# Four cross-attention layers on one core: where the small-head attention groups stand in the order of the program

## The chip, the cores and the metric

The kernel runs on one core of one Trainium2 chip. The metric is the device time of one execution in microseconds (us). Everything is float32. The engines of the core are named as the profile names them: PE (TensorE, matmuls; PEld is its weight load), DVE (VectorE), ACT (ScalarE), POOL (GpSimd) and SP (SyncE, which here only issues DMAs). Each engine works its own instructions in the order of the program and waits for semaphores of others.

## The reference, cut to what matters

Four attention layers follow each other on a state `x` of 4 batches x 512 rows x 256 columns. All four attend to the same context (4 x 1024 x 512). Layers 0, 2 and 3 are alike; layer 1 is another form.

```
# layers 0, 2, 3 ("masked"): 16 heads of 64
q, k, v = x @ Wq, ctx @ Wk, ctx @ Wv
logits  = q k^T / 8 + col_bias        # bias on up to 4 key columns, from two masks over the rows
x       = softmax(logits) v @ Wo + bo + x

# layer 1 ("grouped"): 16 query heads of 16, 4 key/value heads, each shared by 4 query heads
xn      = rmsnorm(x) * norm_w
q, k, v = xn @ wq, ctx @ wk, ctx @ wv
x       = x + softmax(q k^T / 4) v @ wo
```

Layer l+1 of a batch needs layer l of that batch whole; different batches don't depend on each other.

## The kernel before

**Groups.** Work comes in groups (`units`, L44). A masked group is two heads of one layer and one batch: 8 groups a layer, 96 in all. A grouped group of layer 1 is two key/value heads (h = 0 or 1) for one of the four query heads r that share them: 8 for each batch, 32 in all, in the order r0h0, r0h1, r1h0 and so on. For each group 8 tiles of scores, 128 keys x 1024 (two heads x 512 queries), are made, reduced to a maximum over all keys, diminished by it, put through the exponential and multiplied with v.

**Order.** Two strings give the order by hand: character n of `MASKED_TURNS` (L57) is the batch whose next masked group runs in step n, and character n of `GROUPED_TURNS` (L61) is the batch whose next grouped group has its second half in step n, or "." for none. The loop at L1020 runs over the steps n = 0 to 97. In this text step n begins on PE with the first matmul of its masked scores (L692), and steps are told apart by that. In step n there are:

- `g`, the masked group of step n: scores (L692; L698 adds the bias), copied out of PSUM by ACT (L702), maximum by DVE (L706, then `max_quarters` L743 to L758 and `max_everywhere` L769), subtraction on DVE (L777), exponentials on ACT (L783), a running sum of the exponentials on POOL (L822);
- `g1`, the masked group of step n-1: its product with v on PE (`attend`, L722) and `normalise` on DVE (L743 to L868);
- `lam`, the grouped group of step n: subtraction on POOL (L775), exponentials on ACT, its product with v on PE (also L722), `keep_even`/`keep_odd` and, for h = 1, `turn_grouped` (L732 to L839);
- `coming`, the grouped group of step n+1: its scores in four pairs of tiles (`logits_pair`, L669), copied by ACT (L675), maximum by DVE (L681, then as above into L769);
- projections as filling between these: `project_q` (L610), for odd n the keys of the next two masked groups (L514, 32 matmul records in the trace, listed as 8 items by `keys`), for even n their values (L553, 64 records, 8 items by `values`), and `project_out` (L886), whose result DVE adds to the state (L904 or L908). For two masked groups at a time it stands first in the filling of odd steps (`outs`).

So a grouped group has its first half (`coming`) in the step before its own and its second half (`lam`) in its own. In the order before, the 8 grouped groups of a batch stand in consecutive steps (12 to 19, 22 to 29, 32 to 39, 68 to 75), and inside such a block every step has both a `lam` and a `coming`. The step two before a block makes the keys of layer 1 and the norm (`k_grouped` L532, `rms_norm` L649), the step just before it their values (`v_quarter` L576).

**The filling list.** Each entry has a supposed time, which are summed in `now`. Pair 0 of the `coming` scores is put in where `now` reaches 12.0 with a `lam` or 11.0 without; the next three follow 2.5 apart. Before pair 0 `behind_exponentials` sends out everything else that the step still holds: all subtractions, exponentials and `normalise(g1)`. `attend_grouped` (the `lam` product) is put in where 9.5 is reached.

**PSUM.** The 8 banks are given out by `Place` (L101), for one bank or an aligned pair of banks, the longest returned first. This happens in the order of the program, so a matmul that gets a bank waits until the last reader of that bank is done. A pair of grouped score tiles takes two aligned pairs of banks.

**State.** `x_all` (L343) holds four states of 512 KB. A new state is taken when a masked layer's first `project_out` runs and returned when its last `project_q` has run (`new_state`, `drop_state`). `part_x` (L365) loads a batch's input.

**Queue of SP.** All loads of weights and of the context go through SP in program order: `load_masked` at the head of a step, `load_others` at its end. `fetch_half` brings the context of a batch (two halves of 1 MB) when the batch of the masked groups changes.

Of the kernel before, what the change touches and what calls it, by code (L numbers as in the profile page):

```python
# [8 lines left out]
FP = mybir.dt.float32  # L9
# [7 lines left out]
P = 128  # L17
B, S, C = 4, 512, 256
# [3 lines left out]
KC = C // P  # L22
# [21 lines left out]
def units(b):  # L44
# [10 lines left out]


MASKED_TURNS = (  # L57
    "000000001111111122222222000000001111111100000000"
    "222222223333333311111111222222333333332233333333"
)  # L60
GROUPED_TURNS = (  # L61
    "............00000000..11111111..22222222........"
    "....................33333333...................."
)


CONTEXT_STEPS = ((1, 2, 3, 4), (5, 5, 6, 6), (7, 7, 8, 8))


# [11 lines left out]
def kernel(ctx: ExitStack, tc: tile.TileContext, a: dict, out: bass.AP):  # L81
    nc = tc.nc

    def pool(name, **kw):
        return ctx.enter_context(tc.tile_pool(name=name, bufs=1, **kw))
# [3 lines left out]
    dr = pool("dr", space=bass.MemoryType.DRAM)  # L89
# [43 lines left out]
    def give_set(g):  # L133
        sets_free.append(g.set)
# [186 lines left out]
    xs = {}  # L321
# [24 lines left out]
    def new_state(l, b):  # L346
        x_at[l, b] = x_free.pop(0)
        xs[l, b] = x_all[:, x_at[l, b]]
        return xs[l, b]

    def drop_state(l, b):
        x_free.append(x_at[l, b])

    def load_parts(b, first):

# [74 lines left out]
    def w_tile(g, n, kk, bufs):  # L430
        return t_([P, kk, P], f"w{n}", f"w{n}_{g.name}", bufs=bufs)
# [20 lines left out]
    def load_grouped(g, n):  # L452


        if n == "k":
            w = t_([P, NT, P], "v1", f"wk_{g.name}")[:, 0:KT, :]
        else:
            w = t_([P, S], "o1", f"wv_{g.name}").rearrange("p (k c) -> p k c", c=P)
        g.w[n] = w
        nc.gpsimd.memset(w, 0.0)  # L460
        for k in range(KT):
            nc.sync.dma_start(
                out=w[:, k, :].rearrange("p (g d) -> p g d", d=32)[:, :, 0:16],
                in_=a[f"L1_xattn_w{n}"][k * P : (k + 1) * P, :].rearrange("p (g d) -> p g d", d=16),
            )

    def load_q(g):
        if g.masked:
            g.wq = w_tile(g, "q", KC, 2)
            nc.sync.dma_start(  # L470
                out=g.wq,
                in_=a[f"L{g.l}_xattn_Wq"][:, g.p * P : (g.p + 1) * P].rearrange("(k p) c -> p k c", p=P),
            )
        elif g.h == 0:
            g.wq = w_tile(g, "q1", KC, 1)
            nc.gpsimd.memset(g.wq, 0.0)
            for k in range(KC):
                nc.sync.dma_start(
                    out=g.wq[:, k, :].rearrange("p (g d) -> p g d", d=32)[:, :, 0:16],
                    in_=a["L1_xattn_wq"][k * P : (k + 1) * P, :].rearrange(  # L480
                        "p (g r d) -> p g r d", r=4, d=16
                    )[:, :, g.r, :],
                )

    def load_o(g):
        if g.masked or g.h == 1:
            g.wo = t_([P, C], "wo", f"wo_{g.name}", bufs=4)
        if g.masked:
            nc.sync.dma_start(out=g.wo, in_=a[f"L{g.l}_xattn_Wo"][g.p * P : (g.p + 1) * P, :])
        elif g.h == 1:  # L490
            nc.gpsimd.memset(g.wo, 0.0)
            for i in range(4):
                at = 64 * i + 16 * g.r
                nc.sync.dma_start(out=g.wo[32 * i : 32 * i + 16, :], in_=a["L1_xattn_wo"][at : at + 16, :])
# [8 lines left out]
    def k_part(g, n, part):  # L503

        if not g.masked:
            return k_grouped(g, n, part)
        if n == 0 and part == 0:
            g.kt = t_([P, T], "kt", f"kt_{g.name}", bufs=2)
        if part == 0:
            g.k_place = Place(1)  # L510
        w = g.k_place
        m = w.ap
        for k in (2 * part, 2 * part + 1):
            nc.tensor.matmul(  # L514
                m, lhsT=g.w["k"][:, k, :], rhs=ctx_half[g.b, n][:, k, :],
                start=(k == 0), stop=(k == KT - 1),
            )
        if part:
            return lambda: (nc.scalar.copy(g.kt[:, n * 512 : (n + 1) * 512], m), w.back())  # L519
# [188 lines left out]
    def place_out(g, width=1):  # L708
        g.place = Place(width)
        g.po, g.psum = g.place.ap[:, 0:S], g.place.ap[:, S:]  # L710
# [16 lines left out]
    def keep_even(g):  # L727


        if g.h == 0:  # L730
            gq[g.b, "o"] = t_([P, S], "o1", f"o1_{g.name}")
        nc.scalar.copy(gq[g.b, "o"][64 * g.h : 64 * (g.h + 1), :], g.po[0:64, :])  # L732

    def keep_odd(g):
        half = gq[g.b, "o"][64 * g.h : 64 * (g.h + 1), :]
        nc.vector.tensor_tensor(half, half, g.po[64:128, :], ALU.add)  # L736
        g.place.back()
# [86 lines left out]
    def turn_grouped(g):  # L824
        w = Place(1)
        normalise_grouped(g, w.ap)
        w.back()
# [113 lines left out]
    masked = [g for g, _ in steps if g]  # L941
    step_of = {(g.l, g.b, g.u): n for n, both in enumerate(steps) for g in both if g}
# [3 lines left out]
    def at(n):  # L946
        return steps[n] if 0 <= n < len(steps) else (None, None)
# [8 lines left out]
    def head(g):  # L956
        return steps[step_of[1, g.b, 0]][1]
# [8 lines left out]
    for b in range(B):  # L966
        first = next(g for g in masked if (g.b, g.l, g.u) == (b, 0, 0))
        for n, part_of in enumerate(load_parts(b, first.n == 0)):
            at_step = -1
            if first.n:  # L970
                before = masked[first.n - 2]
                at_step = step_of[before.l, before.b, before.u] - 1
                if n < 4:
                    at_step = CONTEXT_STEPS[b - 1][n]
            parts.setdefault(at_step, []).append(part_of)

    def run(items):
# [25 lines left out]
    def keys(*of):  # L1003
        return [
            (1.7, lambda h=h, part=part, each=each: k_part(each, h, part))
            for h in range(2) for each in of for part in range(2)
        ]

    def values(of):
        if of.masked:  # L1010
            return [(1.8, lambda n=n, h=h: v_pair(of, n, h)) for n in range(NI) for h in range(2)]
        return [(1.8, lambda h=h, part=part: part(of, h)) for h in range(2) for part in (v_begin, v_end)]
# [7 lines left out]
    for n in range(len(steps) + 2):  # L1020
        g, lam = at(n)
        follows, coming = at(n + 1)
        soon = at(n + 2)[1]
        g1, attended = attended, g
        ending = n >= len(steps) - 2

        rests = [p() for p in parts.get(n, ())] if n >= 0 else []
        kk = []
        if g:
            kk = masked[1:2] if n == 0 else masked[g.n + 1 : g.n + 3] if g.n % 2 else []  # L1030
# [17 lines left out]
        def load_others():  # L1048
            third = at(n + 3)[1]
            if third and third.first:  # L1050
                load_grouped(third, "k")
            if coming and coming.h == 1 and soon:
                load_q(soon)
            if soon and soon.first:
                load_q(soon)
                load_grouped(soon, "v")
            if coming:
                load_o(coming)
# [80 lines left out]
        if coming:  # L1139
# [6 lines left out]
        fill, of_grouped = (  # L1146
            [
                (1.8 * len(each), lambda each=each: project_out(*each))
                for each in outs if each[0].masked == m
            ]  # L1150
            for m in (True, False)
        )
        outs = []
        fill += [(1.7, lambda each=each: project_q(each)) for each in queries]
        if kk:
            fill += keys(*kk)
        of_values = values(g) if g and g.n % 2 == 0 else []
        fill += of_values[:4] + of_grouped + of_values[4:]
        if lam:

            def attend_grouped():
                while any(of is lam for _, of, _ in events):
                    events.pop(0)[2]()
                lam.v = head(lam).v
                place_out(lam)
                attend(lam)
                give_set(lam)
                late.append(lambda: keep_odd(lam))
                if lam.h == 1:
                    late.append(lambda: turn_grouped(lam))  # L1170
                return lambda: keep_even(lam)

            total, where = 0.0, 0
            while where < len(fill) and total < 9.5:
                total += fill[where][0]
                where += 1
            fill.insert(where, (3.6, attend_grouped))
        if soon and soon.first:
# [5 lines left out]
            of_keys = keys(soon)  # L1184
# [37 lines left out]
        if n == 0:  # L1222
            load_masked()
        load_others()
        for b in range(B):
            if left[b] == 0:
                left[b] = -1
                store(b)
# [23 lines left out]
```

## Time and profile before

| | us |
|---|---|
| median of 3 runs | 3630.98 (3629.69 to 3631.89) |
| the profiled execution, its own time | 3630.16 |
| its span in the trace | 3628.1 |

The mean granted clock of TensorE over the span is 0.995 of full speed. Some groups of the page that the steps are built of, with their mean durations:

| what | engine, line | count | mean ns |
|---|---|---|---|
| subtraction, masked | DVE L777 | 768 | 1215 |
| maximum, masked | DVE L706 | 672 | 1232 |
| maximum, grouped | DVE L681 | 224 | 1233 |
| maximum over a tile's quarters | DVE L743 (scores) | 128 | 1265 |
| spreading the maximum, grouped | DVE L769 | 32 | 1246 |
| adding a projection to the state | DVE L908 | 52 | 1218 |
| copy of a score tile, masked / grouped | ACT L702 / L675 | 768 / 256 | 1048 / 1015 |
| exponential of a tile | ACT L783 | 1024 | 1058 |
| running sum | POOL L822 | 668 | 2365 |
| subtraction, grouped | POOL L775 | 256 | 2371 |

A mean for PE is not the pace at which matmuls follow each other, since they overlap: the chain of waits has stretches of 13.73 us for 32 of L514 (0.429 us each) and 13.81 us for 64 of L553 (0.216 us each). The moving operand of both is float32, with 512 and 256 columns.

### The profile page before, as it was taken

What the parts mean: (1) busy time and instruction counts of PE and PEld (TensorE: products, weight loads), DVE (VectorE), ACT (ScalarE), POOL (GpSimd) and SP (SyncE); (2) the same over time, 40 slices, a digit from 0 to 9 for tenths busy, and PEclk for the clock granted to TensorE, in tenths of its full rate; (3) what the DMA queues carried; (4) which work ended last, traced back from release to release, by engine and by line L of the source; (5) the groups of instructions that cost most, each with busy time, mean ns of one, the idle gap of its engine ahead of it and who ended that gap; (6) DMA issues with size and microseconds to landing.
All of it is one profiled execution on the core that took longest, in us unless ns stands there. A gap on an engine that the chain in (4) does not pass through costs nothing.

```text
span 3628.1 us, 40560 instructions
## 1 busy us (share of the span) xinstructions
PE 3551.9 (98%) x14510; PEld 1708.9 (47%) x14510; DVE 3022.2 (83%) x4134; ACT 2313.0 (64%) x2657; POOL 2220.0 (61%) x1005
## 2 busy tenths in 40 slices
PE   8999999999999999999999999999999999999998
PEld 4554444444444444444545454454444445454554
DVE  7877789887889878998888888888788888888787
ACT  4565577775777667776555555555577765555554
POOL 3565477775677757776555545455577775545454
PEclk9999999999999999999999999999999999999999
DMA  3231101011100110001001001011101101002100
GB/s 89 61 110 62 56 27 41 21 31 43 46 22 22 43 46 22 22 22 42 26 27 50 28 28 50 27 50 30 44 22 46 28 19 50 27 20 71 33 31 6
DMA packets 159373, 140.01 MB, mean 39 GB/s; under 512 B 42424, under 2 KB 142264, under 8 KB 158660
## 3 DMA queue, kind: packets, MB, share of 16 engines
q1 hardware_dynamic: 153518, 124.32, 11.1%
q0 software_dynamic: 2560, 8.39, 0.8%
q10 hardware_dynamic: 3094, 4.72, 0.6%
q8 instruction: 114, 1.87, 0.2%
q14 instruction: 87, 0.71, 0.1%
HBM read 122.71 MB, written 10.49 MB: 37 GB/s over the span
## 4 chain that ended last, share of the span: by engine, by line
PE 72%; DVE 19%; ACT 6%; issue 2%; ACTq 0%; DVEq 0%; DMA 0%; POOL 0%; POOLq 0%
PE ps L514 16%; PE ps L553 15%; PE ps L722 14%; PE ps L692 14%; DVE ps L706 7%; DVE st L777 4%; PE ps L610 4%; PE ps L669 3%; ACT st L783 3%; PE ps L886 3%; DVE ps L743 2%; DVE ps L681 1%; DVE ps L769 1%; ACT st L675 1%; DVE every L758 1%
## 5 line engine op out<-in xcount | busy, mean ns | idle before, releaser
L822 POOL TENSOR_TENSOR st<-st 128x1024 f32<-128x1024 f32 x668 | 1580.0, 2365 | 1058.1 <-ACT st L783 1013.2
L783 ACT ACTIVATE st<-st 128x1024 f32<-128x1024 f32 x1024 | 1035.8, 1058 | 465.9 <-DVE st L777 399.5
L706 DVE TENSOR_TENSOR ps<-ps,st 128x1024 f32<-128x1024 f32 x672 | 828.0, 1232 | 367.9 <-ACT st L702 307.8
L777 DVE TENSOR_TENSOR st<-st,ps 128x1024 f32<-128x1024 f32 x768 | 881.2, 1215 | 3.4
L722 PE MATMUL ps<-st,v 128*64 128x512 f32 (+1 forms) x4064 | 801.5, 595 | 9.2 <-ACT st L783 9.2
L775 POOL TENSOR_TENSOR st<-st 128x1024 f32<-128x1024 f32 x256 | 596.8, 2371 | 313.3 <-DVE st L769 195.7
L702 ACT COPY st<-ps 128x1024 f32<-128x1024 f32 x768 | 716.3, 1048 | 96.5 <-PE ps L698 67.1
L692 PE MATMUL ps<-qt,kt 64*128 64x512 f32 x3072 | 718.1, 599 | 26.4 <-DVE ps L743 19.6
L514 PE MATMUL ps<-ctx,wk 128*128 128x512 f32 x1536 | 695.4, 603 | 2.2 <-ACT ctx L416 2.2
L553 PE MATMUL ps<-wv,ctx 128*128 128x256 f32 x3072 | 687.6, 381 | 0.0
L553 PEld LDWEIGHTS ps<-wv,ctx 128*128 128x128 f32 x3072 | 578.7, 190 | 144.0 <-issue 69.0
L722 PEld LDWEIGHTS ps<-st,v 128*64 128x64 f32 (+1 forms) x4064 | 241.6, 130 | 550.9 <-issue 430.3
L692 PEld LDWEIGHTS ps<-qt,kt 64*128 64x128 f32 x3072 | 300.4, 186 | 386.7 <-issue 147.7
L514 PEld LDWEIGHTS ps<-ctx,wk 128*128 128x128 f32 x1536 | 288.3, 191 | 393.1 <-issue 364.1
L681 DVE TENSOR_TENSOR ps<-ps,st 128x1024 f32<-128x1024 f32 x224 | 276.1, 1233 | 74.2 <-ACT st L675 61.2
L675 ACT COPY st<-ps 128x1024 f32<-128x1024 f32 x256 | 247.5, 1015 | 83.8 <-PE ps L669 82.0
L616 ACT ACTIVATE qt<-ps 128x512 f32<-128x512 f32 x96 | 56.6, 589 | 317.0 <-PE ps L610 317.0
L519 ACT COPY kt<-ps 128x512 f32<-128x512 f32 x192 | 111.2, 579 | 179.3 <-PE ps L514 170.6
L669 PE MATMUL ps<-qt,kt 32*128 32x512 f32 x1024 | 184.4, 645 | 18.7 <-DVE o L736 10.1
L610 PE MATMUL ps<-x,wq 128*128 128x512 f32 x384 | 187.4, 611 | 1.1 <-ACT x L379 1.1
L886 PE MATMUL ps<-ot,wo 128*128 128x512 f32 x384 | 177.9, 606 | 0.7 <-DVE ot L868 0.7
L743 DVE TRANSPOSE_TENSOR_REDUCE ps<-ps 128x32 f32<-128x1024 f32 x128 | 162.0, 1265 | 12.5 <-PE ps L692 0.5
(142 smaller groups left out, 1650.7 us busy)
## 6 DMA issues: line engine op xcount, KB each, us to landing
ctx<-kept SPq DMA_DIRECT2D x24, 1024.0 KB, 8.4
wk<-in_L_xattn_Wk_dram SPq DMA_DIRECT2D x47, 512.0 KB, 3.6
wv<-in_L_xattn_Wv_dram SPq DMA_DIRECT2D x47, 512.0 KB, 3.7
wq<-in_L_xattn_Wq_dram SPq DMA_DIRECT2D x96, 128.0 KB, 3.5
wo<-in_L_xattn_Wo_dram SPq DMA_DIRECT2D x96, 128.0 KB, 3.3
st<-kept SPq DMA_DIRECT2D x4, 2048.0 KB, 9.7
kept<-st SPq DMA_DIRECT2D x12, 512.0 KB, 3.2
qt<-qt ACTq DMA_DIRECT2D x32, 128.0 KB, 2.2
```

Of the source, the lines that this page charges most:

```text
L514: nc.tensor.matmul(m, lhsT=g.w["k"][:, k, :], rhs=ctx_half[g.b, n][:, k, :], start=(k == 0), stop=(k == KT - 1),)
L553: nc.tensor.matmul(m[:, half * 2 * P : (half + 1) * 2 * P], lhsT=ctx_half[g.b, t // 4][:, k, t % 4 * P : (t % 4 + 1) * P], rhs=g.w["v2"][: ...
L610: nc.tensor.matmul(m, lhsT=g.wq[:, k, :], rhs=x[:, k, :], start=(k == 0), stop=(k == KC - 1))
L681: nc.vector.tensor_tensor(top, top, g.st[t], ALU.max)
L692: nc.tensor.matmul(m[:, j * S : (j + 1) * S], lhsT=g.kt[g.rows[j], keys], rhs=g.qt[g.rows[j], :], start=True, stop=t > 0,)
L702: nc.scalar.copy(g.st[t], m)
L706: nc.vector.tensor_tensor(top, top, g.st[t], ALU.max)
L722: nc.tensor.matmul(g.po[at, :], lhsT=g.v[:, t, rows], rhs=g.st[t][:, j * S : (j + 1) * S], start=(t == first), stop=(t == last),)
L775: nc.gpsimd.tensor_tensor(g.st[t], g.st[t], g.mb, ALU.subtract)
L777: nc.vector.tensor_tensor(g.st[t], g.st[t], g.mb, ALU.subtract)
L783: nc.scalar.activation(st, st, AF.Exp)
L822: nc.gpsimd.tensor_tensor(g.acc, g.st[0] if t == 1 else g.acc, g.st[t], ALU.add)
```

## The change

Five things are done.

1. `GROUPED_TURNS`: the first seven grouped groups of a batch stand at every second step, always an even one, and the eighth directly behind the seventh: steps 12, 14, ... 24, 25 for batch 0; 28 to 41 for batch 1; 44 to 57 for batch 2; 60 to 73 for batch 3. So 28 of the 32 steps with a grouped second half have no `coming` of their own; the steps 24, 40, 56 and 72 have both. The `coming` scores stand in odd steps otherwise.
2. `MASKED_TURNS`: some masked layers run in parts of 6 and 2 groups, with groups of another batch between; the batch changes 15 times instead of 12.
3. `AWAY`: eight times an idle state is written to DRAM at the end of a step (`send_away`) and read back at the head of a later one (`bring_back`), 512 KB each way, both on SP.
4. `project_out` of grouped groups moves in odd steps to behind the third of the eight key items, and `attend_grouped` comes after it where both are in one step.
5. The step at which a batch's input is loaded and turned is one later, and `load_q` of a grouped group goes by the group two steps on alone.

```diff
 MASKED_TURNS = (
-    "000000001111111122222222000000001111111100000000"
-    "222222223333333311111111222222333333332233333333"
+    "000000001111111122222222333333000000003300000011"
+    "111111001111112222222211222222333333332233333333"
 )
 GROUPED_TURNS = (
-    "............00000000..11111111..22222222........"
-    "....................33333333...................."
+    "............0.0.0.0.0.0.00..1.1.1.1.1.1.11..2.2."
+    "2.2.2.2.22..3.3.3.3.3.3.33......................"
 )
+AWAY = (
+    (25, 40, 1, 2), (28, 36, 0, 3), (31, 39, 1, 3), (41, 56, 1, 3),
+    (44, 51, 3, 0), (47, 53, 4, 0), (60, 67, 3, 1), (63, 69, 4, 1),
+)
...
+    def send_away(l, b):
+        away[l, b] = dr.tile([P, KC, S], FP, tag=f"away{l}{b}", name=f"away{l}{b}", bufs=1)
+        nc.sync.dma_start(out=away[l, b], in_=xs[l, b])
+        drop_state(l, b)
+
+    def bring_back(l, b):
+        nc.sync.dma_start(out=new_state(l, b), in_=away[l, b])
...
             if first.n:
-                before = masked[first.n - 2]
-                at_step = step_of[before.l, before.b, before.u] - 1
-                if n < 4:
-                    at_step = CONTEXT_STEPS[b - 1][n]
+                at_step = CONTEXT_STEPS[b - 1][n] if n < 4 else first.n - 2
...
+        for _, back, l, b in AWAY:
+            if back == n:
+                bring_back(l, b)
...
-            if coming and coming.h == 1 and soon:
+            if soon and soon.h == 0:
                 load_q(soon)
             if soon and soon.first:
-                load_q(soon)
                 load_grouped(soon, "v")
...
         if kk:
-            fill += keys(*kk)
+            of_keys = keys(*kk)
+            fill += of_keys[:3] + of_grouped + of_keys[3:]
         of_values = values(g) if g and g.n % 2 == 0 else []
-        fill += of_values[:4] + of_grouped + of_values[4:]
+        fill += of_values[:4]
+        if not kk:
+            fill += of_grouped
+        fill += of_values[4:]
...
-            while where < len(fill) and total < 9.5:
+            first_at = max((fill.index(each) + 1 for each in of_grouped), default=0)
+            while where < len(fill) and (total < 9.5 or where < first_at):
...
+        for when, _, l, b in AWAY:
+            if when == n:
+                send_away(l, b)
```

## Prediction

> **What bounds the kernel now.** The page first: PE is busy 98% of the span and the chain that ended last lies mostly on it.
>
> ```profile
> span 3628.1 us, 40560 instructions
> ...
> PE 3551.9 (98%) x14510; PEld 1708.9 (47%) x14510; DVE 3022.2 (83%) x4134; ACT 2313.0 (64%) x2657; POOL 2220.0 (61%) x1005
> ...
> PE 72%; DVE 19%; ACT 6%; issue 2%; ACTq 0%; DVEq 0%; DMA 0%; POOL 0%; POOLq 0%
> ```
>
> A PE that waits inside a run of overlapping matmuls still counts as busy, so I went to single steps: first L692 of one masked group to that of the next, then the busy time in those stretches (columns: stretch, length, busy PE, PEld, DVE, ACT, POOL, granted clock, DMA share, GB/s). In order: step 11 (`coming` alone), 12 and 14 (both, even), 15 (both, odd), 19 (`lam` alone, odd), 31 (`coming` alone), 50 and 51 (masked alone).
>
> ```profile
> 398.30:450.30 52.00, 50.42 (x213) 23.62 (x212) 42.39 (x58) 29.77 (x36) 19.36 (x9) 0.97 0.16 40
> 450.30:490.40 40.10, 39.15 (x199) 20.66 (x198) 32.50 (x42) 33.24 (x40) 32.84 (x16) 1.00 0.01 1
> 541.70:583.10 41.40, 40.65 (x204) 20.95 (x203) 35.76 (x45) 33.78 (x38) 35.73 (x17) 1.00 0.08 22
> 583.10:632.80 49.70, 47.77 (x181) 18.26 (x180) 45.47 (x63) 35.70 (x41) 35.19 (x15) 1.00 0.20 65
> 765.20:804.30 39.10, 38.09 (x143) 15.40 (x142) 35.46 (x53) 26.64 (x31) 32.55 (x14) 1.00 0.07 21
> 1295.10:1346.00 50.90, 48.76 (x211) 22.86 (x210) 42.11 (x57) 30.39 (x38) 20.10 (x9) 1.00 0.25 75
> 2020.00:2050.10 30.10, 30.10 (x137) 18.16 (x136) 25.27 (x35) 18.41 (x21) 12.56 (x6) 1.00 0.15 44
> 2050.10:2083.40 33.30, 33.30 (x111) 13.51 (x110) 27.32 (x38) 18.12 (x21) 19.66 (x10) 1.00 0.07 24
> ```
>
> Masked steps stand on PE (30.03 and 33.38 us, nothing lost). In step 15 DVE is busy 45.5 of 49.7: that step is DVE's, and its PE waits some 7.5 us. Steps 11 and 31 are what odd steps with grouped scores will look like: they hold no `lam`, DVE has 10 us to spare, and PE waits all the same. The timeline of step 31 shows for what:
>
> ```profile
> 1322.90 1.13 PE L669 MATMUL ps<-qt,kt 32*128 32x512 f32 x4 [0.18 <-DVE st L777]
> ...
> 1326.49 0.69 DVE L868 TENSOR_TENSOR ot<-ps,ot 128x512 f32<-128x512 f32 x1
> ...
> 1327.23 1.14 PE L669 MATMUL ps<-qt,kt 32*128 32x512 f32 x8 [1.29 <-DVE ot L868]
> ```
>
> Pair 0 waits for the last subtraction (the maximum's banks), pair 1 for `scale_out` (the bank of `g1`): the queue on DVE in front of the pairs counts, not DVE's sum. The timeline at the head of step 19 shows the wait after late pairs: the maximum of the grouped scores still holds two banks.
>
> ```profile
> 767.13 1.26 DVE L743 TRANSPOSE_TENSOR_REDUCE ps<-ps 128x32 f32<-128x1024 f32 x1
> ...
> 768.45 3.45 PE L692 MATMUL ps<-qt,kt 64*128 64x512 f32 x13 [1.01 <-DVE ps L743]
> ```
>
> **The order of the groups (1), priced by new kinds of step.** Offsets (+) are from the step's start. Without waits the timeline gives PE: a key item 1.72, 1.91 behind a pair; a pair 1.07; `project_q` 1.72; grouped `project_out` 1.75; `lam` product 3.57.
>
> *Even, `lam` alone, behind an h=0 score step (E0):* 30.03 + 3.57 and 0.1 of switching = 33.7. POOL needs 8 x 2.37 = 19.0 for the subtractions from about +2.4, so +21.4; the product stands at +24.85 as in step 12, covered. The 16.6 of running sums then end at +38, some 4 us into the next step, where `normalise` reads them at +27: covered.
>
> *Odd, scores h=1 (S1):* as step 31 up to the end of its keys at +41.22, without the norm that step has at its head: DVE's first maximum starts there at +4.00, in masked step 51 at +3.40, so DVE's chain is 0.6 earlier. Four key items end at +26.5; pair 0 waits for the last subtraction (+27.2), ends +28.3; a key item, +30.1; pair 1 waits for `scale_out` (+31.5), ends +32.6; the rest as in step 31. 40.6.
>
> *Even, `lam` behind it (E1):* only one key item (1.8) follows the last pair, DVE frees its banks at +3.2 of this step as in step 19: the wait at its head, 2.0. 35.7.
>
> *Odd, scores h=0 (S0), where part 4 counts:* two `project_q` and three key items end at +26.4. Pair 0 as in step 11, 0.6 earlier: first half at +27.5, second at +28.75 behind the copy of the keys on ACT, end +29.8. ACT's exponentials end at +30.6 (31.23 in step 11), the two copies of pair 0 at +32.45. Directly behind pair 0 now stands the grouped `project_out`, PE to +31.6. It takes two banks; the open third key item holds one, the running maximum two. Handing out the banks by `Place`, pair 1 is left with exactly the pair just copied and the pair of this projection. The latter comes back when DVE has added it, behind `normalise` (+31.7) and pair 0's maximum (+32.5 to 33.7): 1.22 more, +34.95. So half of pair 1 goes at +32.5, half at +35.0, end +35.6, instead of +32.7 right behind the projection. Then 1.85, pair 2, 1.9, pair 3 to +41.4, three key items, 5.3. **46.7**, of which 5.1 are waiting. In steps 39, 55 and 71 a `project_q` comes last, the projection stands ahead of pair 0, and the same working gives 45.1.
>
> *Step F+12* (both, even) 40.1 as step 12; *F+13* (`lam` alone, odd) 39.1 as step 19; F the block's first step.
>
> Per batch, F to F+13: 3 x 33.7 + 3 x 40.6 + 3 x 35.7 + 3 x 46.7 + 40.1 + 39.1 = 549.3. Before: the blocks took 354.0, 356.2, 354.4 and 356.0 (mean 355.2), and the six masked steps that they now mix with 3 x 63.41 = 190.2; together 545.4. So +3.9 a batch, **+15.6**; less 3 x 1.6 for steps 39, 55, 71, **+10.8**. Steps F-2 and F-1 stay. The gain is real (an E step loses 0.1 to 2 where both-steps lost 3 to 8), but the pairs' waits, paid 4 times for a block's first scores, are now paid 28 times.
>
> **The clock.** In step 11 PE's longest gap is 1.50, yet the granted clock halves just after (columns as above):
>
> ```profile
> 425.80:429.20 3.40, 2.78 (x9) 1.01 (x10) 3.15 (x11) 3.38 (x5) 3.24 (x3) 1.00 0.13 28
> 429.20:432.60 3.40, 3.40 (x8) 1.18 (x10) 2.53 (x3) 2.67 (x4) 3.32 (x2) 0.50 0.00 0
> ```
>
> Such windows follow in three of the four steps ahead of a block (11, 21, 67) and in two of the twelve odd steps inside. [...] By the row, one halved window costs up to 1.7. The trace decides: 9 S0 x 0.4 x 1.3 (part hidden in the waits) and 12 S1 x 0.15 x 1.5: **+7**; ends 0 and 24 x 1.7 = 41.
>
> **Idle states (3).** No 512 KB write and read back of a state is in the trace; nearest are `kept<-st`, 3.2 us to landing, and `kept<-ctx`, 4.8. Each state is back a step before it is read (nearest: read back at step 36, used by the `project_q` in step 37), its slot is returned a step before, and the DMA engines are busy under 0.25 in these stretches. A send waits on SP for the last `project_out` addition (about +22 of its step); behind it are the next step's loads, whose weights are first read 14 us into that step. Between 0 and 8 x 4 = 32 if a wait showed; nothing is removed, so not below 0. I take 0, as no step shows a PE wait on SP's loads.
>
> **Parts of layers (2).** Three more changes of batch, six more loads of 1 MB (8.4 us each to landing); two end some 17 us after the odd step's start, the keys that read them stand at +19.5. Step 47, with such a load, takes 33.38 like its neighbours: 0; without that cover up to 3 x 5 = 15. **The rest (5)** moves a 0.97 us run of transposes from an odd step to an even one and four small loads: 0.
>
> **Sum.** 3628.1 + 10.8 + 7 = 3646 span; the profiled execution's own time is 2.1 above its span, the median 0.8 above that: 3648.
>
> **Rivals.**
> *A, not slower:* pair 1 of S0 does not wait for the addition. For it: DVE idles between maxima in step 11 (0.80, 1.94), so its queue may be earlier. Against it: DVE works in order behind `normalise`. The point is the addition's end: at +33 or earlier instead of +34.95, S0 is 44.0, 9 x 2.7 = 24 less: 3617 to 3624 with and without clock windows. From S0 = 44.7 it is no slower.
> *B, the clock* halves in every odd score step: 3630 + 11 + 41 = 3682. For: 3 of 4 in the likest steps; against: 2 of 12 inside blocks.
> *C, SP:* the sends and returns hold up loads: 3648 + 32 = 3680. Against: the covers above.
> *D, the spreading takes away all pair waits:* S0 41.6, S1 38.3, E1 33.7, 9.4 less for four steps, twelve times: about 3530. For: DVE's sum of 68 us fits in 75; against: steps 11 and 31.
>
> **Chances.** Forecast 0.58 (3631 to 3672), A 0.17, B 0.13, C 0.08, D 0.04. 0.2% (7.3 us) is about what a measurement can tell from no change: faster 0.17 (D, most of A, a little of the forecast), within 0.17, slower 0.66. The range 3612 to 3684 leaves out D and the tails.
>
> **What would show it.** In step 15 of the changed kernel: L669's second pair released by DVE's addition (L908's line), 46 to 47 us; steps 13 and 17 near 40.6; step 14 near 35.7 with an L692 wait of 2; step 16 near 33.7; halved clock windows near the pairs. S0 below 44.7, or a PE wait on a DMA at steps 36 to 69, makes it wrong.

## The result, and the profile after

| | before | changed |
|---|---|---|
| median, us | 3631.2 (3629.69 to 3631.89) | 3672.23 (3669.50 to 3674.29) |
| span of the profiled execution, us | 3628.1 | 3670.3 |
| windows of 3.41 us in which PE's clock is halved (granted clock 0.50), between the first and the last step | 6 | 17 |

The changed kernel takes 1.0113 times as long, 95% interval 1.0096 to 1.0131: 41 us slower where 17 were forecast. Halved windows, here and below, are counted in the one profiled execution of each kernel. The head of the page and its chain hardly tell why:

```profile
span 3670.3 us, 40647 instructions
...
PE 3572.4 (97%) x14510; PEld 1702.5 (46%) x14510; DVE 3020.9 (82%) x4134; ACT 2310.3 (63%) x2657; POOL 2219.8 (60%) x1005
...
PE 72%; DVE 21%; ACT 4%; issue 2%; ACTq 0%; DMA 0%; DVEq 0%; POOL 0%; POOLq 0%
```

No compute engine has more instructions. DVE, ACT and POOL are busy as long as before; PE is busy 20.5 us longer with the same 14510 matmul records, and the rest of the 42 us is waiting. The new kinds of step do show, in the busy time by stretch of the changed kernel (columns as before: stretch, length, busy PE, PEld, DVE, ACT, POOL, granted clock, DMA share, GB/s). These are step 13 (scores, h=1), 16 (second half behind h=0), 18 (second half behind h=1), and steps 35 and 47, both scores with h=0:

```profile
484.30:525.00 40.70, 39.41 (x145) 14.96 (x144) 33.64 (x42) 25.64 (x29) 21.05 (x10) 1.00 0.07 22
610.20:644.00 33.80, 33.80 (x169) 18.97 (x168) 28.45 (x42) 25.98 (x30) 30.90 (x14) 1.00 0.08 24
685.00:720.70 35.70, 34.36 (x169) 18.94 (x168) 33.85 (x51) 26.49 (x31) 29.36 (x13) 1.00 0.07 23
1377.40:1427.70 50.30, 47.67 (x153) 17.78 (x152) 38.44 (x49) 27.04 (x31) 22.66 (x11) 0.93 0.12 33
1865.70:1912.90 47.20, 44.57 (x153) 16.84 (x152) 38.42 (x49) 27.04 (x31) 22.64 (x11) 1.00 0.12 35
```

The first three stand where they were forecast (40.6, 33.7, 35.7), the last within 0.5 (46.7). Step 35 is the same work as step 47 and takes 3.1 more at a clock of 0.93. The timeline of step 47 has the wait of pair 1:

```profile
1895.46 1.98 PE L898 MATMUL ps<-o,wo 128*128 128x512 f32 x4
...
1897.93 1.23 DVE L693 TENSOR_TENSOR ps<-ps,st 128x1024 f32<-128x1024 f32 x1 [0.76 <-ACT st L687]
1897.95 1.13 PE L681 MATMUL ps<-qt,kt 32*128 32x512 f32 x4 [0.50 <-ACT st L687]
1899.07 1.21 DVE L920 TENSOR_TENSOR x<-ps,x 128x1024 f32<-128x1024 f32 x1
...
1900.34 1.13 PE L681 MATMUL ps<-qt,kt 32*128 32x512 f32 x4 [1.26 <-DVE x L920]
```

The grouped projection (L898) runs, half of pair 1 follows once ACT has copied pair 0, and the other half stands until DVE has been through pair 0's maximum (L693) and the addition (L920). In step 35 the same wait ends in two windows of half clock:

```profile
1408.20:1411.60 3.40, 2.11 (x7) 0.45 (x5) 2.63 (x3) 2.17 (x3) 3.32 (x2) 1.00 0.00 0
1411.60:1418.40 6.80, 6.33 (x12) 2.19 (x16) 2.79 (x3) 1.79 (x3) 3.14 (x2) 0.50 0.00 0
```

PE was busy 2.11 of 3.40 us, no gap over 1.3, and the next 6.8 us ran at half speed. The last section has what sets this step apart from step 47 in the trace.

### The profile page after: what moved, and what is told of

It reads as the page before. It is cut to its first block, busy times and chain, and to the rows that moved or that the text cites. A ratio compares the mean times of both kernels' runs of the same rounds, so it can differ in the third digit from the quotient of the medians.

```text
span 3670.3 us, 40647 instructions
## 1 busy us (share of the span) xinstructions
PE 3572.4 (97%) x14510; PEld 1702.5 (46%) x14510; DVE 3020.9 (82%) x4134; ACT 2310.3 (63%) x2657; POOL 2219.8 (60%) x1005
## 4 chain that ended last, share of the span: by engine, by line
PE 72%; DVE 21%; ACT 4%; issue 2%; ACTq 0%; DMA 0%; DVEq 0%; POOL 0%; POOLq 0%
PE ps L565 18%; PE ps L734 16%; PE ps L704 13%; PE ps L526 13%; DVE ps L718 7%; DVE st L789 5%; PE ps L622 4%; PE ps L681 4%; PE ps L898 2%; DVE ps L755 2%; DVE ps L693 1%; ACT st L714 1%; ACT st L795 1%; DVE ps L781 1%; ACT st L687 1%
## 5 line engine op out<-in xcount | busy, mean ns | idle before, releaser
L734 PE MATMUL ps<-st,v 128*64 128x512 f32 (+1 forms) x4064 | 790.1, 595 | 0.0
L704 PE MATMUL ps<-qt,kt 64*128 64x512 f32 x3072 | 716.3, 601 | 29.9 <-DVE ps L755 18.9
L526 PE MATMUL ps<-ctx,wk 128*128 128x512 f32 x1536 | 709.7, 609 | 2.2 <-ACT ctx L428 2.2
L704 PEld LDWEIGHTS ps<-qt,kt 64*128 64x128 f32 x3072 | 289.6, 186 | 399.3 <-ACT st L714 147.0
L693 DVE TENSOR_TENSOR ps<-ps,st 128x1024 f32<-128x1024 f32 x224 | 275.9, 1232 | 114.6 <-ACT st L687 104.0
L681 PE MATMUL ps<-qt,kt 32*128 32x512 f32 x1024 | 199.7, 657 | 44.3 <-DVE ot L880 18.0
L572 ACT COPY v<-ps 128x512 f32<-128x512 f32 x192 | 110.1, 575 | 125.2 <-PE ps L565 124.9
L898 PE MATMUL ps<-ot,wo 128*128 128x512 f32 x384 | 177.9, 605 | 0.7 <-DVE ot L880 0.7
```

The lines of the kernel that those rows point to most:

```text
L526: nc.tensor.matmul(m, lhsT=g.w["k"][:, k, :], rhs=ctx_half[g.b, n][:, k, :], start=(k == 0), stop=(k == KT - 1),)
L681: nc.tensor.matmul(ws[odd].ap[:, j * S : (j + 1) * S], lhsT=g.kt[rows, i * P : (i + 1) * P], rhs=g.qt[rows, :], start=True, stop=True,)
L704: nc.tensor.matmul(m[:, j * S : (j + 1) * S], lhsT=g.kt[g.rows[j], keys], rhs=g.qt[g.rows[j], :], start=True, stop=t > 0,)
L734: nc.tensor.matmul(g.po[at, :], lhsT=g.v[:, t, rows], rhs=g.st[t][:, j * S : (j + 1) * S], start=(t == first), stop=(t == last),)
```

## The experiments

**Part 4 undone.** The grouped projection goes behind all key items again.

```diff
-            of_keys = keys(*kk)
-            fill += of_keys[:3] + of_grouped + of_keys[3:]
+            fill += keys(*kk)
```

> Undoes part 4 alone: grouped project_out stands behind all eight key items of an odd step again; order of groups, parts of layers and DRAM states stay as changed. Theory (pair 1 of the scores with h=0 waits for DVE's addition of this projection, and the clock halves on top in steps 19, 23, 31 and 35): that wait goes, the twelve such steps take about 44.6 us instead of 45.3 to 50.5 (572.5 in sum, so 38 less), 3634 us in all (3628 to 3645). Rival (the loss comes from the parts of layers and the states sent to DRAM, or from spreading as such): these steps stay above 47 and the time stays over 3660.

Measured: 3643.68 us, 1.0035 times before (1.0022 to 1.0047), so 28.5 less than the changed kernel. The twelve steps take 44.1 to 46.1, 538.8 in sum instead of 572.5, and the halved windows fall from 17 to 6. Ten us more than forecast are left, seven of them since the wait for the addition isn't quite gone: it stands at the head of the next step now (L704, the masked scores), which takes 34.4 to 34.6 instead of 33.8. The theory holds for the wait. The waits of the changed kernel show it by name on L681 (first three lines); this kernel has no such line on L681, but the one on L704 (last line):

```profile
PE ps L681 <- DVE ot L880: 18.0, 14, 1.3
PE ps L681 <- DVE st L789: 16.0, 16, 2.3
...
PE ps L681 <- DVE x L920: 7.3, 9, 1.3
```

```profile
PE ps L704 <- DVE x L920: 5.0, 12, 0.5
```

(Waiter, releaser, us in total, times, longest.) The nine waits on L681 stand once in each of the h=0 steps but 39, 55 and 71.

**Part 1 undone.** Parts of layers and stored states stay.

```diff
-    "............0.0.0.0.0.0.00..1.1.1.1.1.1.11..2.2."
-    "2.2.2.2.22..3.3.3.3.3.3.33......................"
+    "............00000000........11111111........2222"
+    "2222........33333333............................"
```

> Undoes part 1 alone: the eight grouped groups of a batch stand in consecutive steps again (12 to 19, 28 to 35, 44 to 51, 60 to 67); parts of layers, batch changes and the sixteen DMAs of states stay as changed. Theory (states and parts cost nothing, all of the loss comes from the spread steps): 3631 us, give or take 6, with masked steps at 30.0 and 33.4 and no PE wait on a DMA. Rival (states and parts cost): 3655 or more, with waits at the steps where a state is sent or read back.

Measured: 3635.74 us, 1.0012 (1.0004 to 1.0021). Masked steps take 30.03 and 33.38. The trace has nine halved windows, three more than before; steps 29, 45 and 61, where five of them stand, take 53.4 to 55.0 instead of 50.4. All that stays changed here, the parts, the sixteen DMAs and the place of the projection within the blocks, costs some 4 us together (1.5 to 8 by the interval), of a change of 41. And the changed kernel's PE waits for a DMA only in the start-up, 5.5 us in all where it was 5.1 before.

**PE kept busy in the wait.** Two more matmuls behind each grouped `project_out` of an odd score step, into a bank that nobody reads.

```diff
+        if busy_after:
+            w2 = Place(1)
+            for n in range(busy_after):
+                nc.tensor.matmul(w2.ap, lhsT=g.wo[:, 0:P], rhs=g.ot, start=n == 0, stop=n == busy_after - 1)
+            w2.back()
```

> The changed kernel with two more matmuls (4 records, 1.7 us) behind each grouped project_out of an odd score step, into a free bank that nothing reads: they fill PE's wait for the addition. Theory (the halved clock windows are caused by PE's waits at pair 1 and cost what steps 19, 23, 31 and 35 take over the 47.2 of the others, 11.4 in all): the windows at +34 go, all nine such steps take 47.2, steps 39, 55 and 71 one us more each, 3663 us (3657 to 3667). Rival (the clock costs nothing beyond waits that are there anyway, or halves regardless): 3672 to 3680.

Measured: 3659.52 us, 1.0078 (1.0061 to 1.0095). With 48 matmul records more the kernel is 12.7 us faster. Halved windows fall from 17 to 7, and none of the seven stands behind a filled wait; three stand at +30, ahead of it. Steps 19, 23, 31 and 35 take 47.2 to 47.7 instead of 49.0 to 50.5, step 15 takes 0.5 more. The clock's part in the loss is measured by that: 9.8 us in the nine h=0 steps other than 39, 55 and 71, and 1.8 in the steps F+13 (25, 41, 57 and 73), where one of two windows is gone too.

**Pairs later.** On top of part 4 undone, pairs start one key item later.

```diff
-            pairs += [((12.0 if lam else 11.0) + 2.5 * i, i) for i in range(NT // 2)]
+            pairs += [((12.0 if lam else 12.5) + 2.5 * i, i) for i in range(NT // 2)]
```

> As e1_proj_last, and pairs of scores in steps without a grouped second half are put in from 12.5 of the supposed time instead of 11.0, so one key item later. Theory (pair 0 waits for the last subtraction and pair 1 for scale_out, both on DVE): the h=0 steps lose 1.7 more (42.9), the h=1 steps take 38.7 instead of 40.7 but the step behind them 37.5 instead of 35.7, as its head waits longer for the banks of the maximum: 17 us below e1_proj_last, 3617. Rival (the waits only move to the head of the next step in both kinds): equal to e1_proj_last within 5 us.

Measured: 3648.21 us, 1.0048 (1.0031 to 1.0065). The rival held: h=0 steps lose 1.2 and the steps behind them gain 1.7; h=1 steps lose 0.5 and the steps behind them gain 0.7. The wait went to the next step's head.

**The maximum's banks taken later.** To test the wait at a step's head on the kernel before, and on the one with part 4 undone.

```diff
-        g.mx_place.back()
+        g.mx_place.back(3 if not g.masked else 0)
```

> The kernel before, with one edit: the two banks of a grouped group's maximum count as returned three places later, so that the masked scores of the next step take another pair of banks third and these banks fifth. Nothing else moves. Theory (the 2.0 to 2.8 us wait at the head of 16 steps is a wait for these banks until DVE has reduced them at +3.2): the wait shrinks by 1 to 1.3 us each, 16 to 21 us in all, 3612 us (3605 to 3620). Rival (ACT's copies of the score tiles set the pace there, so that with two banks fewer in turn the same time is lost): within 5 us of before.

> e1_proj_last with the same edit of the return of the grouped maximum's banks. Theory: the head waits behind the h=1 score steps (2.0, twelve), in F+13 (2.8, four) and behind the h=0 ones (0.6 to 0.9, nine) shrink by about 1.2, 1.2 and 0.5: 24 us below e1_proj_last, 3620. Rival (ACT sets the pace): equal to e1_proj_last within 5 us.

Measured: 3643.41 us, 1.0032 (1.0020 to 1.0045), and 3673.60, 1.0118 (1.0101 to 1.0134): 12 and 30 slower than without the edit. Theory and rival were both wrong. The timeline of the second at the head of step 14:

```profile
527.95 1.26 DVE L755 TRANSPOSE_TENSOR_REDUCE ps<-ps 128x32 f32<-128x1024 f32 x1
...
529.92 0.77 DVE L770 TENSOR_TENSOR every<-ps,other_max 32x32 f32<-32x32 f32 x4
...
530.74 0.70 PE L704 MATMUL ps<-qt,kt 64*128 64x512 f32 x2 [2.42 <-DVE every L770]
```

The pair now taken third holds the small work bank of the same reduction, which is read until L770, 2 us later than L755. And behind the longer single wait the clock is halved more often: 16 and 14 windows instead of 6 in each, 18 of the 30 of them 4 to 7 us into such a step.

**A shorter queue on DVE.** `normalise` left out in the odd score steps, on top of part 4 undone; this kernel leaves out the division there.

```diff
-            late.append(lambda: normalise(g1))
+            late.append(lambda: (leave_undivided if coming and not lam else normalise)(g1))
```

> e1_proj_last, but in odd steps with grouped scores and no grouped second half the masked product is copied without its division by the sum of exponentials (normalise left out there: the output is not the reference's), so DVE's queue ahead of the pairs is 3.6 us shorter. Theory (pair 1 of the h=1 scores waits for scale_out at the end of that queue, its other banks being free at +30.6): these twelve steps lose 1.0 each, the h=0 steps nothing as they wait for ACT's copies: 12 us less than e1_proj_last, 3631. Rival (the waits are ACT's in both kinds): no change within 4 us; or (DVE is the bound of these steps): 3.6 x 28, about 100 us less.

Measured: 3628.94 us, 0.9995 (0.9986 to 1.0003), 14.7 less than with the division. The h=1 steps take 39.7 instead of 40.7, as step 17 of this kernel; its waits have no line on L880 any more:

```profile
639.20:678.90 39.70, 39.70 (x143) 15.29 (x142) 30.40 (x32) 25.73 (x29) 20.75 (x10) 1.00 0.07 21
```

```profile
PE ps L681 <- ACT st L687: 12.5, 13, 1.0
PE ps L681 <- DVE st L789: 2.2, 4, 1.2
```

Taking 3.6 us of DVE out of a step gives 1.0. So these steps are not bound by DVE's sum: pair 1 waited for `scale_out`, and the longest waits left are those for ACT's copies. In the profiled execution seven h=0 steps also had a halved window at +33 and took 46.5.

**Another bank for `normalise`.** So that pair 1 of the h=1 steps need not wait, with the division kept.

```diff
-                at = min(free, key=lambda n: free[n] + (2 if n ^ 1 in free else 0))
+                at = min(free, key=lambda n: free[n] + (2 if n ^ 1 in free else 0) + (99 if n == spare else 0))
...
-        w = Place(1)
+        w = Place(1, g.place.banks[0] ^ 1)
         reciprocal_sums(g, w.ap)
```

> e1_proj_last with one bank given out otherwise: the work bank of normalise is not the other half of the pair that holds the masked product, so that the next key item finds that half free and pair 1 of the h=1 scores gets a pair of banks that doesn't wait for scale_out. Theory: as where normalise was left out, the twelve h=1 steps take 39.7 instead of 40.65, nothing else moves: 12 us below e1_proj_last, 3632, give or take the clock windows (5). Rival (DVE's queue as such is the wait): no change.

Measured: 3675.68 us, 1.0121 (1.0106 to 1.0137), 32 slower than without. The theory fell: pair 1 no longer waits for `scale_out`, but pair 0 now waits twice, once for each of its halves. In nine of the twelve h=1 steps these waits are 0.6 to 0.8 us (for a subtraction) and 0.4 us (for a copy of keys on ACT), 1.0 to 1.2 in sum where one wait of 1.3 stood. In steps 29, 45 and 61 the second is 1.4 us, as pair 0 got the bank there that `normalise` works in:

```profile
PE ps L681 <- ACT kt L531: 6.6, 12, 0.9
...
PE ps L681 <- DVE short L864: 4.3, 3, 1.4
```

Busy time of steps 13, 33 and 29 of this kernel:

```profile
486.10:527.00 40.90, 39.84 (x145) 14.96 (x144) 33.65 (x42) 25.76 (x29) 21.06 (x10) 1.00 0.08 23
1290.98:1333.67 42.69, 41.50 (x143) 15.49 (x142) 33.73 (x43) 25.59 (x29) 20.75 (x10) 0.96 0.07 21
1131.20:1176.10 44.90, 42.82 (x143) 15.86 (x142) 33.68 (x42) 25.75 (x29) 21.43 (x10) 0.92 0.19 66
```

Where the clock holds, step 13, nothing is lost or won (40.9 for 40.7). Step 33 has the same kinds of wait, 1.2 us in sum, and takes 1.8 more than step 13 with one halved window. Step 29 has the longer wait and two windows. Steps 39, 55 and 71 have two windows each as well and take 48.3 to 48.6 for 44.1. The trace has 23 halved windows.

**Two DMAs off ACT's queue.** `project_q` copies a grouped query twice and doubles each by a DMA that ACT issues. In the kernel before, ACT stands still for some 0.55 us behind such an issue (L621), ahead of the exponentials and copies that the score pairs wait for.

```diff
-                    nc.scalar.dma_start(out=g.qts[h][there, :], in_=g.qts[h][here, :])
+                    nc.sync.dma_start(out=g.qts[h][there, :], in_=g.qts[h][here, :])
```

Tried with the other bank, on the kernel before, with part 4 undone, and on the changed kernel:

> e12_bank, and the two small DMAs that double a grouped query (L633 of the changed kernel) are issued by SP instead of ACT. ACT's two pauses of 0.55 us behind them stand ahead of the exponentials and the copies that pair 0 and pair 1 of the h=0 scores wait for. Theory: the twelve h=0 steps and the four ahead of a block lose about 1.1 each: 16 us below e12_bank, 3616, below the kernel before. Rival (DVE's subtractions set the exponentials' pace anyway, or SP's queue holds up loads behind these two): 3632 or more.

> The kernel before with the two DMAs that double a grouped query issued by SP instead of ACT. Theory: its sixteen steps with a grouped project_q lose up to 1.1 each, the odd steps inside blocks less as POOL feeds their exponentials: 3620 (3613 to 3629). Rival: 3631 within 3.

> e1_proj_last with the two DMAs that double a grouped query issued by SP instead of ACT (without the other bank of e12_bank). Theory: the twelve h=0 steps take 43.8 instead of 44.8 and more, the four ahead of a block 1 to 2 less, the clock halves in at most five windows: 3626 us (3620 to 3636), still above the same edit on the kernel before (3614), because the spread order pays the waits of the score pairs in 28 steps. Rival (spreading is better once these pauses are gone): 3614 or less.

> The changed kernel with the same two DMAs on SP. Theory: pair 1 of the h=0 scores still waits for DVE's addition, whose queue is less than 1 us earlier, so these steps take 46.4 to 47 where the clock isn't halved: 12 us less than the changed kernel from the pauses, and whatever the halved windows do on top: 3655 (3645 to 3668). Rival (ACT's pauses are the whole wait of the h=0 steps): 3630 or less.

| | us | against before (95%) | halved windows |
|---|---|---|---|
| other bank, part 4 undone | 3647.58 | 1.0050 (1.0036 to 1.0064) | 9 |
| **kernel before** | **3613.97** | **0.9957 (0.9944 to 0.9971)** | 5 |
| part 4 undone | 3626.67 | 0.9988 (0.9981 to 0.9994) | 3 |
| changed kernel | 3654.91 | 1.0066 (1.0052 to 1.0079) | 9 |

The edit is worth 28, 16, 17 and 17 us on the kernels it was put on. The first stays far from the 3616 expected for it, as the bank's edit below it had cost 32 instead of gaining 12; its halved windows fall from 23 to 9. The last three came within 6 us of what was expected. The timelines of the kernel before and of this version, ACT in step 15, show the pause and that it is gone:

```profile
611.02 0.60 ACT L620 ACTIVATE qt<-ps 64x512 f32<-64x512 f32 x1 [0.54 <-ACT qt L620]
611.65 0.47 ACTq L621 DMA_DIRECT2D qt<-qt  x1
...
612.16 1.06 ACT L783 ACTIVATE st<-st 128x1024 f32<-128x1024 f32 x1 [0.55 <-ACT qt L620]
```

```profile
605.71 1.20 ACT L620 ACTIVATE qt<-ps 64x512 f32<-64x512 f32 x2
606.32 1.14 SPq L621 DMA_DIRECT2D qt<-qt  x2
606.93 2.95 ACT L783 ACTIVATE st<-st 128x1024 f32<-128x1024 f32 x3
```

The kernel before with this one line changed is the fastest of all, 16 us below before and 58 below the changed kernel. With the same edit and part 4 undone, the spread order is 12.7 us behind it, with fewer halved windows (3 against 5). The parts and states cost some 4 of that by their own experiment, so spreading as such loses here.

## Why the prediction was right in kind and wrong in size

The sign, the place and the mechanism held: pair 1 of the h=0 scores waits for the addition. But 41 us came where 17 were forecast (42 against 18 in the spans). Two terms of the sum failed: the clock, put at +7, took 15.5 us in the new kinds of step, and the four steps F+13 at the end of the blocks took 5.5 more than the 156.4 forecast even without the clock. By the prediction's steps:

- *Kinds of step.* Sums over all steps of a kind, forecast and measured: twelve h=1 score steps 487.2 and 488.9; twelve behind them 428.4 and 432.3; twelve behind h=0 404.4 and 405.6; the three of 45.1 135.3 and 136.0; F+12 160.4 and 161.0. Right, but for steps 14 and 22, which took 2 us more each for the transposes of a new batch's input, a run that I had moved at no cost ("the rest (5)": 0, measured 4).
- *S0, 46.7.* Forecast 420.3 for nine, measured 436.5. The wait for the addition is as described, and shown by undoing part 4. Where the clock costs nothing, the step takes 47.2 (4.4 in nine); the other 11.8 are the clock.
- *F+13, 39.1.* Forecast 156.4 for four, measured 165.3. The row taken for it, step 19, follows a step whose pairs end earlier. Behind a step like 12 the wait at the head is 2.8, not 2.0, as step 13 of the kernel before has it. Two of the four also hold the output's transposes (1.3 each), and two a halved window (1.7 each).
- ***The clock: +7.*** This term failed by a factor of two. It had 4 of 10 h=0 steps halved, 0.15 of the h=1 steps and none of F+13. The trace has windows in eight of the nine h=0 steps (11.8 us), in step 55 (0.3), in two of F+13 (3.4) and in no h=1 step. The mean price of a halved h=0 step, 1.5 us, was near the 1.3 of the sum; the chance was not. One step's windows cost anything between 0 (steps 51, 63 and 67: halved at +30 while PE waits, 47.2 as in step 47) and 3.3 (steps 23, 31 and 35: halved at +34 for two windows, over pair 1 and the key items behind it).
- *Parts, states: 0.* Right within the 4 us that undoing the spreading left.

So of the 24.4 us missed in the span 8.5 are the clock's (15.5 less 7), 5.5 F+13's without it, 4.4 S0's, 4 the transposes of steps 14 and 22, and 4 small excesses of the new steps. In the other direction the rest of the kernel took 1.8 less than the sum had for it. The rivals A (pair 1 doesn't wait), C (DMAs) and D (no waits) fell. B, the clock, was part of the truth, not in every step.

What was open in the prediction, what sets the steps in which the clock is halved apart from others of the same shape, can be read from the traces; the last section has the working. It was found in the traces of all these runs, and no run was made to test it.

## What to carry to other kernels

Before moving work into a step, hand out its buffers on paper in program order: the cost of the moved projection was not its 1.75 us on PE but the two banks that it held until another engine's queue came round to it. Price a spread order by the wait that each step pays once, not by the engine sums that it evens out: here 28 steps that wait for their scores lost against 4 such steps and 28 fuller ones. And look for idle time that an engine gives itself ahead of the chain that counts, as the two DMA issues on ACT: that line was worth more than all the reordering.

## What the runs showed of the hardware

In the traces of the kernel before and of the changed one PE's clock is halved for one or two windows of 3.41 us at a time between the first and the last step, and in every trace all changes of the granted clock lie on one grid of 3.413 us: in the kernel before it falls to 0.50 at 429.20 and is back at 432.61, and falls again at 876.35, 131 of these windows after the first fall. What goes with a halving here is how much matmul work falls between two points of this grid. To see it, add up the matmul records of such a stretch: each counts 0.429 us for 512 float32 columns, the pace measured for L514, times the share of the 128 rows that it uses (the bfloat16 bias at half). The paces of the changed kernel behind this count: two records on 64 rows of L704 stand 0.429 us ahead of the next two, two of the bias on 64 rows of L710 0.216. Here are PE's lines for the same wait in two such stretches of the changed kernel, 1408.24 to 1411.65 in step 35, which is followed by a halved one, and 1896.35 to 1899.76 in step 47, which is not:

```profile
1407.73 1.45 PE L898 MATMUL ps<-o,wo 128*128 128x512 f32 x3
1409.68 1.13 PE L681 MATMUL ps<-qt,kt 32*128 32x512 f32 x4 [0.50 <-ACT st L687]
```

```profile
1896.00 1.45 PE L898 MATMUL ps<-o,wo 128*128 128x512 f32 x3
1897.95 1.13 PE L681 MATMUL ps<-qt,kt 32*128 32x512 f32 x4 [0.50 <-ACT st L687]
```

The records of the projection follow each other at 0.43 us (L898). In step 35 the grid leaves 0.78 us of them in the stretch, in step 47 0.94; the four records on 32 rows count a quarter each, 0.43 together. So the sums are 1.21 and 1.37 us. In the traces of the kernel before and the changed one together, from the start of step 1 to that of the last one and at full clock, all 14 stretches with a sum below 1.23 us are followed by a halved one, 4 of the 7 between 1.23 and 1.40, and none of the 2028 above. Over all fourteen traces it is each of 97, 20 of 47, and 1 of 14191. PE's busy time and its longest gap don't tell them apart: in the changed kernel a stretch with 1.64 us busy and a gap of 1.77 (at 2916.9) is not followed by a halved one, and one with 2.73 busy and no gap over 0.54 (at 2049.9) is, as most of its time goes to eight records on 32 rows. So steps of the same shape fall on either side by where the grid cuts their waits, as steps 35 and 47 do with 1.21 and 1.37 us. A limit near 1.3 us is an estimate from these counts, for this kernel; no run tested it.

Waits that are short but close together were enough for a halving here: between the first and the last step of the changed kernel the longest gap of PE is 2.31 us, and the clock cost 15.5 us in the new kinds of step. In the experiment with another bank, waits that were split in two, and longer in three steps, gave 23 windows for 6 and cost 32 us; 48 needless matmul records in a wait took 10 windows and 12.7 us away.

And ACT paused where it issued a DMA: in the kernel before it stood still some 0.55 us behind 25 of its 32 issues in L621, and issuing all 32 from SP took 16 us off.
